# An LSTM over diagonals: x products of short diagonals made together, row buffers kept, two powers in one instruction

## The chip, the cores and the metric

The kernel runs on one core of one Trainium2 chip. The metric is the device time of one execution in microseconds. The kernel before was timed three times: 3999.95, 4003.45 and 4011.36 us, median 4003.45.

TensorE is called PE in the profile (PEld are its weight loads), VectorE is DVE, ScalarE is ACT, GpSimd is POOL and SyncE is SP, which here only issues DMAs. All data is fp32.

## What is computed

The reference takes an image batch of 16 x 64 x 64 positions with 128 features. Layer 0 normalises x over groups of 4 features and runs a two-dimensional LSTM over the 64 x 64 positions; its output is added to x. Layer 1 (attention with landmarks, then a recurrence over tokens) follows and isn't touched by the change. The LSTM step, cut to its core:

```python
f0 = sigmoid(x @ wf0 + bf0 + h_u @ uf0)      # h_u, c_u: the position above
f1 = sigmoid(x @ wf1 + bf1 + h_l @ uf1)      # h_l, c_l: the position to the left
hsum = h_u + h_l
it = sigmoid(x @ wi + bi + hsum @ ui)
ot = sigmoid(x @ wo + bo + hsum @ uo)
cp = tanh(x @ wc + bc + hsum @ uc)
c = f0 * c_u + f1 * c_l + it * cp
h = ot * tanh(c)
```

A position needs those above and to its left, so all positions of one diagonal can be computed at once, and diagonals follow one another.

## The kernel before

**Units.** `lstm_grid` (lines 142 to 372) goes over the 127 diagonals. A diagonal of n positions has 16 n columns (positions times batch); features lie on the 128 partitions. The batch is split in two halves of 8 (`HB`). Up to n = 32 both halves make one unit of 16 n columns; longer diagonals make two units of 8 n columns, so that one half's products can run while the other half's gates are computed. That gives 190 units, numbered 0 to 189 here: units 0 to 31 are diagonals 0 to 31, units 32 to 157 the halves of diagonals 32 to 94, units 158 to 189 diagonals 95 to 126. [...]

**Products.** Each of five gates needs a product with x (`gate_x`, L240) and one with h or with the sum of two h (`gate_h`, L244), added in one PSUM tile `ls_z`. In fp32 a product is two matmul records in the trace, so a unit has ten x records and ten h records. ACT applies the gate's function from `ls_z` (L246).

**Rows of x.** Positions of a diagonal are loaded (`load`, L218) as rows of 128 features, up to 16 positions times 8 images on the 128 partitions, in up to four tiles a unit. Tiles begin at multiples of 16 positions; from diagonal 64 on the first position needed (`lo`) often lies inside a tile, and POOL then clears that tile (L217) before the load, which fills only the rows needed. `enter` transposes the rows on PE (L225), DVE subtracts the group mean (L228) and POOL multiplies by the group's inverse deviation (L232), which gives `ls_xn`, the input of the x products.

**The slot.** The order on every engine is written by hand (`tc.manual_schedule`): `slot(t)` (L319) issues, in this order: the load of unit t + AHEAD (5); h products and gates of unit t; DVE's statistics of the finished rows of unit t - 2 (`measure`, L263, L264); the cell of unit t, with one product on POOL (L330) and the rest on DVE (L329, L331 to L333), tanh on ACT (L334); the transposes of unit t - 1's h back to rows with x added (`turn`, L255, L257); the new h (L338) and the sums of states for the next unit (L236); POOL's factors of unit t - 2 (`factors`, L272 to L282); `enter` of unit t + 2; ACT's normalisation of unit t - 3 (L287) and its stores (L295 on SP); the sum of unit t - 4 for the landmarks (`collect`, L302); the x products of unit t + 1. Each engine runs its part in that order. So on POOL a slot is: L330 of unit t, L272 to L282 of unit t - 2, L232 of unit t + 2, and the clearing (L217) for the next load.

**Factors.** Each row is normalised twice in later layers. `factors` computes, for the k tiles of a unit (2 to 4), the variance plus epsilon (L272), a second value from it (L273), and their powers of -0.5 (L274, L275: a tensor_tensor with the exponents from a constant tile `mhalf`); then, for late units, a mask that zeroes the factor of rows outside the band, one instruction for each such tile (L279), and a bias (L281, L282).

**Before the LSTM** `group_stats` (L34) reads all of x for the group means and deviations. It calls a list of jobs, one an image from the fourth image on: a first job of the attention's tables, the loads of the first units (on ACT's DMA queue), seven more jobs of tables, and at last the turning of a weight (L745 to L750). The 16 images leave room for 13 jobs; there are 12. The last images' statistics end in a short chain over ACT (L81) and POOL (L82, L83) that gives `grstd`.

Of the kernel before, what the change touches and what calls it, by code (L numbers as in the profile page):

```python
# [8 lines left out]
F32 = mybir.dt.float32  # L9
AF = mybir.ActivationFunctionType  # L10
ALU = mybir.AluOpType
# [4 lines left out]
P = 128  # L16
# [4 lines left out]

AHEAD = 5
EPS = 1e-5
# [84 lines left out]
def lstm_tiles(nc, cp, shape, w, u, bias):  # L108

    B, D0, F = shape  # L110
    S = 2
    HB = B // S
    KT = D0 * HB // P
    wt, ut, bt = [], [], []
    for g in range(5):
        a = cp.tile([P, P], F32, name=f"ls_w{g}")
        nc.scalar.dma_start(out=a, in_=w[g])
        wt.append(a)
        a = cp.tile([P, P], F32, name=f"ls_u{g}")
        nc.scalar.dma_start(out=a, in_=u[g])  # L120
        ut.append(a)
        a = cp.tile([P, 1], F32, name=f"ls_b{g}")
        nc.scalar.dma_start(out=a, in_=bias[g].rearrange("(p o) -> p o", o=1))
        bt.append(a)

    hs = [cp.tile([P, S, D0 + 1, HB], F32, name=f"ls_h{k}") for k in range(2)]
    cs = [cp.tile([P, S, D0 + 1, HB], F32, name=f"ls_cell{k}") for k in range(2)]
    for a in (*hs, *cs):
        nc.vector.memset(a, 0.0)
    rows = [cp.tile([P, KT, 2 * F + 4], F32, name=f"ls_tt{k}") for k in range(7)]  # L130
    for a in rows:
        nc.vector.memset(a[:, :, F : F + 4], 1.0)

    later = cp.tile([P, P // HB], F32, name="ls_later")
    nc.gpsimd.memset(later, 1.0)
    nc.gpsimd.affine_select(
        out=later, in_=later, compare_op=ALU.is_ge, fill=0.0, base=0, pattern=[[-HB, P // HB]], channel_multiplier=1
    )
    return wt, ut, bt, hs, cs, rows, later


def lstm_grid(nc, tc, x, fixed, ld, stats, ident, mhalf, gmean, grstd, t1, acc):

# [15 lines left out]
    with ExitStack() as ctx:  # L159
        wt, ut, bt, hs, cs, rows, later = fixed  # L160

# [3 lines left out]
        def unit(t, d, s0, s1):  # L165
# [23 lines left out]
            v.cu, v.cl, v.co = part(before, v.lo), part(before, v.lo + 1), part(now, v.lo + 1)  # L189
            v.tt = rows[t % len(rows)]  # L190
            v.z, v.a = {}, {}
            return v

        def view(v, a):

            return a[:, : v.cols].rearrange("p (s x) -> p s x", s=v.ns)

        def span(v, s, i, c):

            n = (v.hi - v.base) * HB  # L200
            return slice((s - v.s0) * n + (i - v.base) * HB, (s - v.s0) * n + (i - v.base + c) * HB)
# [10 lines left out]
        def load(v, eng=nc.sync):  # L212
            v.xt = ld.tile([P, KT, F], F32, tag="xt", name="ls_xt")
            for k, s, i, c in v.tiles:
                rows, cells = inner(v, i, c)
                if rows.start:
                    nc.gpsimd.memset(v.xt[:, k, :], 0.0)  # L217
                eng.dma_start(out=v.xt[rows, k, :], in_=xv[cells, s * HB : s * HB + HB])  # L218

        def enter(v):  # L220

            xp = ps_t.tile([P, NC], F32, tag="xp", name="ls_xp")
            for k, s, i, c in v.tiles:
                q = c * HB
                nc.tensor.transpose(xp[:, span(v, s, i, c)], v.xt[:q, k, :], ident[:q, :q])  # L225
            v.xn = wk.tile([P, NC], F32, tag="xn", name="ls_xn", bufs=4)[:, : v.cols]
            a = v.xn.rearrange("p (s c b) -> p s c b", s=v.ns, b=HB)
            nc.vector.tensor_tensor(  # L228
                a, xp[:, : v.ns * (v.hi - v.base) * HB].rearrange("p (s c b) -> p s c b", s=v.ns, b=HB)[:, :, v.lo - v.base :],
                norm(v, gmean), ALU.subtract,  # L230
            )
            nc.gpsimd.tensor_tensor(a, a, norm(v, grstd), ALU.mult)  # L232

        def add_states(v):
            v.hsum = view(v, wk.tile([P, NC], F32, tag="hsum", name="ls_hsum"))
            nc.vector.tensor_add(v.hsum, v.hu, v.hl)  # L236

        def gate_x(v, g):
            v.z[g] = ps_z.tile([P, NC], F32, tag="z", name="ls_z")
            nc.tensor.matmul(v.z[g][:, : v.cols], wt[g], v.xn, start=True, stop=False)  # L240

        def gate_h(v, g):
            hin = (v.hu, v.hl)[g] if g < 2 else v.hsum
            nc.tensor.matmul(view(v, v.z[g]), ut[g], hin, start=False, stop=True)  # L244
            a = wk.tile([P, NC], F32, tag=f"g{g}", name=f"ls_g{g}", bufs=3)
            nc.scalar.activation(a[:, : v.cols], v.z[g][:, : v.cols], AF.Tanh if g == 4 else AF.Sigmoid, bias=bt[g])  # L246
            v.a[g] = view(v, a)

# [17 lines left out]
        def factors(v):  # L266
# [6 lines left out]
            nc.gpsimd.tensor_scalar(ve[:, 1, :k], var, 1.0 + EPS, EPS * EPS, ALU.mult, ALU.add)  # L273
            nc.gpsimd.tensor_tensor(v.tt[:, 0:k, F + 2], ve[:, 0, :k], mhalf[:, :k], ALU.pow)  # L274
            nc.gpsimd.tensor_tensor(v.tt[:, 0:k, F + 3], ve[:, 1, :k], mhalf[:, :k], ALU.pow)  # L275
            for j, s, i, c in v.tiles:
                if i < v.lo:
                    f = v.tt[:, j, F + 3 : F + 4]
                    nc.gpsimd.tensor_tensor(f, f, later[:, v.lo - i : v.lo - i + 1], ALU.mult)  # L279
            v.nb = sm.tile([P, KT], F32, tag="nb", name="ls_nb")  # L280
# [24 lines left out]
        for d in range(D0 + D1 - 1):  # L305
# [3 lines left out]
            for s0, s1 in halves:  # L309
# [4 lines left out]
                ready.setdefault(t, []).append(v)  # L314

        def get(t):
            return units[t] if 0 <= t < len(units) else None

        def slot(t):  # L319
            v, p1, p2, p3, p4, after, nxt = (get(t + j) for j in (0, -1, -2, -3, -4, 1, 2))  # L320
            if far := get(t + AHEAD):
# [19 lines left out]
            if p2:  # L341
                factors(p2)
            if nxt:
                enter(nxt)
            if p3:
                normalise(p3)
                store(p3)
            if p4:
                collect(p4)
            if after:  # L350
                for g in (0, 1, 2, 4, 3):
                    gate_x(after, g)

        with tc.manual_schedule(
# [9 lines left out]
            ps_t = ctx.enter_context(tc.tile_pool(name="ls_pst", bufs=1, space=PSUM, reuse_waits="tile"))  # L364
            for t in range(2):
                enter(units[t])
            for r in ready[-1]:
                add_states(r)
            for g in (0, 1, 2, 4, 3):
                gate_x(units[0], g)  # L370
            for t in range(len(units) + 4):
                slot(t)
# [1078 lines left out]
def kernel(ctx: ExitStack, tc: tile.TileContext, ins: dict, out: bass.AP):  # L1451
# [25 lines left out]
    with tc.tile_pool(name="at_c", bufs=1) as ac, tc.tile_pool(name="at_x", bufs=1) as xp, tc.tile_pool(  # L1477
# [4 lines left out]
        with tc.tile_pool(name="first", bufs=1) as first:  # L1482
# [3 lines left out]
            lw = [[ins[f"L0_conv_{k}{g}"] for g in GATES] for k in "wub"]  # L1486
            with tc.tile_pool(name="ls_c", bufs=1) as lc, tc.tile_pool(name="ls_ld", bufs=AHEAD + 4) as ld:
                start = ExitStack()
# [12 lines left out]

                lstm_grid(nc, tc, x, lstm_fixed, ld, stats, ident, mhalf, gmean, grstd, t1, acc)
            rows = [load_rows(nc, xp, t1, 0, g) for g in range(3)]
# [29 lines left out]
```

## Time and profile before

| what | us |
|---|---|
| median of three runs | 4003.45 |
| the profiled execution, its own time | 4009.5 |
| its span | 4008.0 |
| LSTM in the span | about 109 to 1446 |
| PE busy in the span | 3773.7 (94%) |
| POOL busy | 2902.2 (72%) |
| DVE busy | 3012.7 (75%) |
| ACT busy | 2501.7 (62%) |
| POOL's powers L274, 190 instructions | 224.6 |
| POOL's clearing L217, 120 instructions of 0.204 | about 24 |

The span is the time from the first to the last instruction of the profiled execution; 1.5 us of its time lie around it. Rows of instructions in order of time give start, length, engine, line, operation, tile written and tiles read, shape, count, and in brackets the idle time before it with what ended it. Waits are listed as who waited for whom: microseconds in total, times, longest. Rows of matmuls overlap in the profile (their ends are modelled), so short stops of PE show only in the distance between starts.

### The profile page before, as it was taken

The page shows a single profiled execution, that of the slowest core. Times are in us where ns is not written, and L with a number is a line of the kernel's source. Part 1 is how long each engine was busy: PE and PEld are TensorE (multiplying, and loading weights), DVE is VectorE, ACT ScalarE, POOL GpSimd, SP SyncE. Part 2 cuts the span into 40 slices and gives each one's busy share as a digit, 9 for nine tenths or more (in the row PEclk, how much of TensorE's full clock was granted, in tenths as well). Part 3 has the DMA queues.
Part 4 walks back from the last instruction along what each step waited for, and adds up shares of the span by engine and source line. Part 5 has one row for each costly group of instructions (what it writes and reads, how often), then busy time and mean ns, then how long its engine had stood idle before and what let it go on. Part 6 is the DMA issues. An engine that isn't in the chain of part 4 may idle for free. (4 is left out here: it accounts for less than half of the span.)

```text
span 4008.0 us, 98643 instructions
## 1 busy us (share of the span) xinstructions
PE 3773.7 (94%) x36906; PEld 2555.1 (64%) x36906; DVE 3012.7 (75%) x7378; ACT 2501.7 (62%) x5131; POOL 2902.2 (72%) x4440
## 2 busy tenths in 40 slices
PE   7999999999999879889999999999999999988697
PEld 5857655555676669556666666666666666654476
DVE  8689988778888864337788888878888778757465
ACT  0566566566665644346777777677777777645597
POOL 0688877788998954148888888888888888876133
PEclk9899999999999979899999999999999999989799
DMA  9123332323332200113333333333333333223799
GB/s 348 50 73 84 82 82 81 84 83 91 89 86 77 74 17 5 42 28 82 93 85 93 93 86 93 89 88 95 85 91 93 85 95 85 82 65 91 240 266 178
DMA packets 500468, 383.80 MB, mean 96 GB/s; under 512 B 35976, under 2 KB 466960, under 8 KB 499984
## 3 DMA queue, kind: packets, MB, share of 16 engines
q1 hardware_dynamic: 477588, 340.85, 29.5%
q0 software_dynamic: 17728, 34.61, 4.8%
q8 instruction: 294, 4.82, 0.5%
q10 hardware_dynamic: 4668, 1.98, 0.2%
q14 instruction: 190, 1.56, 0.1%
HBM read 172.82 MB, written 204.48 MB: 94 GB/s over the span
## 5 line engine op out<-in xcount | busy, mean ns | idle before, releaser
L984 POOL TENSOR_TENSOR at_total<-at_total,at_e 128x512 f32<-128x512 f32 x480 | 611.6, 1274 | 119.6 <-ACT at_e L957 89.1
L246 ACT ACTIVATE ls_g<-ls_z,ls_b 128x304 f32<-128x304 f32 (+26 forms) x950 | 489.0, 545 | 229.4 <-PE ls_z L244 195.3
L240 PE MATMUL ls_z<-ls_xn,ls_w 128*128 128x304 f32 (+26 forms) x1900 | 607.1, 467 | 8.7 <-POOL ls_xn L232 8.2
L240 PEld LDWEIGHTS ls_z<-ls_xn,ls_w 128*128 128x128 f32 x1900 | 340.4, 196 | 190.7 <-issue 85.7
L851 POOL TENSOR_SCALAR at_T<-at_T,at_nb 128x128 f32<-128x128 f32 x512 | 403.7, 796 | 13.3
L920 DVE TENSOR_REDUCE at_mxq<-at_bank 128x1 f32<-128x512 f32 x512 | 327.6, 682 | 82.6 <-PE at_bank L917 82.4
L244 PE MATMUL ls_z<-ls_hsum,ls_u 128*128 128x304 f32 (+26 forms) x1140 | 371.1, 462 | 0.0
L957 ACT ACTIVATE at_e<-at_bank 128x512 f32<-128x512 f32 x512 | 264.4, 602 | 115.7 <-PE at_bank L951 112.9
L1039 DVE TENSOR_REDUCE at_cmx<-at_bank 128x8 f32<-128x512 f32 x512 | 317.4, 683 | 18.1 <-PE at_bank L1032 14.8
L1068 ACT ACTIVATE at_eT<-at_bank 128x512 f32<-128x512 f32 x512 | 264.4, 602 | 74.4 <-PE at_bank L1065 74.3
L244 PEld LDWEIGHTS ls_z<-ls_hsum,ls_u 128*128 128x128 f32 x1140 | 213.3, 196 | 128.6 <-issue 76.9
L244 PE MATMUL ls_z<-ls_h,ls_u 128*128 128x304 f32 (+26 forms) x760 | 260.6, 466 | 17.3 <-DVE ls_h L338 17.2
L334 ACT ACTIVATE ls_g<-ls_cell 128x304 f32<-128x304 f32 (+26 forms) x190 | 93.2, 491 | 282.1 <-DVE ls_cell L333 278.5
L287 ACT ACTIVATE ls_tt<-ls_tt,ls_nb 128x128 f32<-128x128 f32 (+9 forms) x632 | 261.1, 479 | 5.6 <-POOL ls_nb L282 5.6
L330 POOL TENSOR_TENSOR ls_g<-ls_g,ls_cell 128x304 f32<-128x304 f32 (+26 forms) x190 | 182.1, 958 | 97.7 <-ACT ls_g L246 73.7
L1339 DVE SCALAR_TENSOR_TENSOR rc_y<-rc_w,rc_scale,rc_z 128x256 f32<-128x256 f32 x344 | 155.3, 480 | 108.4 <-PE rc_z L1326 107.0
L274 POOL TENSOR_TENSOR ls_tt<-ls_ve,mhalf 128x4 f32<-128x4 f32 (+2 forms) x190 | 224.6, 1182 | 15.2
L1326 PE MATMUL rc_z<-rc_y,rc_vT 128*128 128x256 f32 x688 | 185.6, 406 | 42.0 <-ACT rc_y L1347 29.6
L1120 ACT ACTIVATE at_z<-at_u,at_nb,at_r 128x128 f32<-128x128 f32 x512 | 211.6, 505 | 11.9 <-POOL at_nb L1115 11.9
L331 DVE TENSOR_TENSOR ls_g<-ls_g,ls_g 128x304 f32<-128x304 f32 (+26 forms) x190 | 98.4, 518 | 159.4 <-POOL ls_g L330 155.5
L1320 POOL DMA_DIRECT2D out_dram<-rc_tt x64 | 77.4, 1209 | 190.5 <-ACT rc_tt L1317 188.6
L244 PEld LDWEIGHTS ls_z<-ls_h,ls_u 128*128 128x128 f32 x760 | 141.6, 196 | 110.3 <-issue 51.0
(262 smaller groups left out, 9696.4 us busy)
## 6 DMA issues: line engine op xcount, KB each, us to landing
t<-ls_tt SPq DMA_DIRECT2D x392, 130.0 KB
at_T<-t SPq DMA_DIRECT2D x128, 264.0 KB
gs_xb<-in_x_dram SPq DMA_DIRECT2D x64, 512.0 KB
at_xh<-t SPq DMA_DIRECT2D x128, 256.0 KB
t<-at_u SPq DMA_DIRECT2D x128, 256.0 KB
out_dram<-at_u SPq DMA_DIRECT2D x128, 256.0 KB
wx<-at_fx SPq DMA_DIRECT2D x128, 256.0 KB
rc_w<-wx SPq DMA_DIRECT2D x64, 512.0 KB
```

Of the source, the lines that this page charges most:

```text
L240: nc.tensor.matmul(v.z[g][:, : v.cols], wt[g], v.xn, start=True, stop=False)
L244: nc.tensor.matmul(view(v, v.z[g]), ut[g], hin, start=False, stop=True)
L246: nc.scalar.activation(a[:, : v.cols], v.z[g][:, : v.cols], AF.Tanh if g == 4 else AF.Sigmoid, bias=bt[g])
L274: nc.gpsimd.tensor_tensor(v.tt[:, 0:k, F + 2], ve[:, 0, :k], mhalf[:, :k], ALU.pow)
L287: nc.scalar.activation(v.tt[:q, k, F + 4 :], v.tt[:q, k, 0:F], AF.Identity, bias=v.nb[:q, k : k + 1], scale=v.tt[:q, k, F + 3 : F + 4],)
L851: nc.gpsimd.tensor_scalar(x[:, c, :], x[:, c, :], gr.nbt[:, 0, c : c + 1], gr.nbt[:, 1, c : c + 1], ALU.mult, ALU.subtract)
L920: nc.vector.tensor_reduce(gr.im.mxq[:, n : n + 1, gr.g], gr.s[n], AX.X, ALU.max)
L957: nc.scalar.activation(gr.e[:, n].rearrange("p c m -> p (c m)"), s[n], AF.Exp)
L984: nc.gpsimd.tensor_tensor(total, total, e[:, :, c, :], ALU.add)
L1039: nc.vector.tensor_reduce(gr.mx[:, n].rearrange("p j c -> p c j"), gr.s[n].rearrange("p (c j m) -> p c j m", c=C, j=2), AX.X, ALU.max)
L1068: nc.scalar.activation(gr.eT[:, n], s[n], AF.Exp)
L1120: nc.scalar.activation(gr.z[:, c, :], gr.u[:, c, :], AF.Identity, bias=gr.nb[:, c : c + 1], scale=gr.r3[:, c : c + 1])
```

## The change

- **x products together.** Neighbouring units whose columns sum to 512 or less are bundled, up to four: diagonals 0 to 3, 4 to 7, 8 to 10, 11 and 12, 13 and 14 at the start; 111 and 112, 113 and 114, 115 and 116, 117 to 119, 120 to 123, 124 to 126 at the end. All other units stay alone. The first unit of a bundle holds the `ls_xn` and `ls_z` tiles for all; its x products are made once for all columns, in the slot before it. Each unit's h product adds to its own columns. So that x is there in time, the units of a bundle enter one in each slot, the last of them two slots before the bundle begins, and loads run 7 units ahead instead of 5. Before the first slot four units enter instead of two; the list of jobs of `group_stats` has one job of loads more, 13 in all.
- **Row buffers kept.** The rows of x go to eleven buffers that are cleared once on POOL before the loop; L217 goes away.
- **Powers.** L274 and L275 become one instruction over both values; the masks of a unit's tiles (L279) become one instruction.

```diff
-AHEAD = 5
+AHEAD = 7
...
+    xs = [cp.tile([P, KT, F], F32, name=f"ls_xt{k}") for k in range(AHEAD + 4)]
+    for a in xs:
+        nc.gpsimd.memset(a, 0.0)
...
         def load(v, eng=nc.sync):
-            v.xt = ld.tile([P, KT, F], F32, tag="xt", name="ls_xt")
             for k, s, i, c in v.tiles:
                 rows, cells = inner(v, i, c)
-                if rows.start:
-                    nc.gpsimd.memset(v.xt[:, k, :], 0.0)
                 eng.dma_start(out=v.xt[rows, k, :], in_=xv[cells, s * HB : s * HB + HB])
...
         def gate_x(v, g):
             v.z[g] = ps_z.tile([P, NC], F32, tag="z", name="ls_z")
-            nc.tensor.matmul(v.z[g][:, : v.cols], wt[g], v.xn, start=True, stop=False)
+            nc.tensor.matmul(v.z[g][:, : v.total], wt[g], v.xn[:, : v.total], start=True, stop=True)

         def gate_h(v, g):
             hin = (v.hu, v.hl)[g] if g < 2 else v.hsum
-            nc.tensor.matmul(view(v, v.z[g]), ut[g], hin, start=False, stop=True)
+            z = v.first.z[g][:, v.off : v.off + v.cols]
+            nc.tensor.matmul(view(v, v.first.z[g]), ut[g], hin, start=False, stop=True, skip_group_check=True)
...
-            nc.gpsimd.tensor_tensor(v.tt[:, 0:k, F + 2], ve[:, 0, :k], mhalf[:, :k], ALU.pow)
-            nc.gpsimd.tensor_tensor(v.tt[:, 0:k, F + 3], ve[:, 1, :k], mhalf[:, :k], ALU.pow)
-            for j, s, i, c in v.tiles:
-                if i < v.lo:
-                    f = v.tt[:, j, F + 3 : F + 4]
-                    nc.gpsimd.tensor_tensor(f, f, later[:, v.lo - i : v.lo - i + 1], ALU.mult)
+            nc.gpsimd.tensor_tensor(
+                v.tt[:, 0:k, F + 2 : F + 4], ve[:, :, :k].rearrange("p r k -> p k r"),
+                mhalf[:, : 2 * k].rearrange("p (k r) -> p k r", k=k), ALU.pow,
+            )
+
+            first = [j for j, s, i, c in v.tiles if i < v.lo]
+            if first:
+                f = v.tt[:, first[0] : first[-1] + 1 : max(first[-1] - first[0], 1), F + 3]
+                r = v.lo - v.base
+                nc.gpsimd.tensor_tensor(f, f, later[:, r : r + 1].to_broadcast([P, len(first)]), ALU.mult)
...
+        while t < end:
+            k = 1
+            while k < 4 and t + k < end and sum(v.cols for v in units[t : t + k + 1]) <= NC:
+                k += 1
+            for j, v in enumerate(units[t : t + k]):
+                v.first, v.off = units[t], sum(p.cols for p in units[t : t + j])
+                if not t:
+                    continue
+                now = entering.setdefault(t + j - k - 1, [[]])
+                if sum(p.ns * (p.hi - p.base) for p in (*now[-1], v)) * HB > NC:
+                    now.append([])
+                now[-1].append(v)
...
-            if nxt:
-                enter(nxt)
+            if t in entering:
+                for vs in entering[t]:
+                    enter(vs)
...
-            if after:
+            if after and after is after.first:
                 for g in (0, 1, 2, 4, 3):
                     gate_x(after, g)
...
-            for t in range(2):
-                enter(units[t])
+            enter(bundle)
             for r in ready[-1]:
                 add_states(r)
             for g in (0, 1, 2, 4, 3):
                 gate_x(units[0], g)
+            for t in range(-AHEAD, 0):
+                for vs in entering.get(t, ()):
+                    enter(vs)
```

## The prediction

> **What bounds the kernel now.** I read the page first, then the busy time of each engine in stretches of the span, then the waits of those stretches, then the order of time. The change touches only the LSTM, which runs from 109 to 1446 us of the span, so that stage alone is priced.
>
> Busy time by stretch (length; PE, PEld, DVE, ACT, POOL; granted clock; DMA):
>
> ```profile
> 109.00:141.00 32.00, 30.81 (x146) 28.42 (x146) 12.81 (x62) 11.47 (x38) 12.49 (x35) 0.52 0.03 7
> ...
> 307.00:540.00 233.00, 232.62 (x942) 160.09 (x942) 219.12 (x616) 139.09 (x329) 193.22 (x289) 1.00 0.32 84
> 540.00:1154.00 614.00, 614.00 (x2096) 348.75 (x2095) 499.95 (x1316) 388.07 (x745) 519.64 (x702) 1.00 0.31 85
> 1154.00:1242.00 88.00, 83.29 (x370) 62.78 (x369) 74.05 (x215) 51.22 (x130) 80.92 (x148) 1.00 0.32 88
> ...
> 1330.00:1425.00 95.00, 78.95 (x450) 64.82 (x448) 74.83 (x262) 58.33 (x161) 86.30 (x208) 1.00 0.24 65
> ```
>
> PE never idles from 540 to 1154 us. POOL is busy 92% of 1154 to 1242 and 91% of 1330 to 1425, where PE does idle. A busy PE hides short stops, because the rows of matmuls overlap; so I also took the starts of PE's rows in order of time. A slot runs from one unit's first h product (L244) to the next's. Its work is ten h records and ten x records (L240) at their usual pitch, plus the transposes at 0.109 us; what is left is a stop. Units are numbered 0 to 189. The stops sum to: units 0 to 5, 1.1 us; 6 to 13, 6.2; 14 to 31, 2.1; 32 to 66, 5.2; 67 to 143, 2.5; 144 to 157 (1154 to 1242 us), 8.5; 158 to 168, 0; 169 to 188 (1330 to 1437 us), 21.6. In all 47 us could be won by removing stops; the rest of the LSTM is PE's own work. Who causes them is in the waits of 1154 to 1242 and then of 1330 to 1437 (total, times, longest):
>
> ```profile
> PEld ls_z L240 <- POOL ls_xn L232: 8.0, 14, 1.0
> ```
> ```profile
> DVE ls_g L331 <- POOL ls_g L330: 18.0, 21, 1.4
> PE ls_z L244 <- DVE ls_h L338: 13.6, 18, 1.0
> ```
>
> In the first stretch PE waits for POOL's normalised x (L232). In the second it waits for the state h, because DVE waits for POOL's product (L330), which stands in POOL's queue behind the factors of an older unit. POOL in order of time there, one unit of 1385 to 1391 us:
>
> ```profile
> 1384.23 0.82 POOL L274 TENSOR_TENSOR ls_tt<-ls_ve,mhalf 128x2 f32<-128x2 f32 x1
> 1385.03 0.88 POOL L275 TENSOR_TENSOR ls_tt<-ls_ve,mhalf 128x2 f32<-128x2 f32 x1
> 1385.99 0.80 POOL L279 TENSOR_TENSOR ls_tt<-ls_tt,ls_later 128x1 f32<-128x1 f32 x2
> ...
> 1387.34 0.74 POOL L232 TENSOR_TENSOR ls_xn<-ls_xn,grstd 128x176 f32<-128x176 f32 x1
> 1388.02 0.34 POOL L217 MEMSET ls_xt<- 128x128 f32 x2
> 1388.32 0.58 POOL L330 TENSOR_TENSOR ls_g<-ls_g,ls_cell 128x192 f32<-128x192 f32 x1
> ```
>
> No idle time stands in front of any of them: POOL sets the pace, and the change shortens just this queue.
>
> **What POOL saves per unit.** No power of 2k elements beside another is in the trace for k = 3 or 4 tiles, but these rows give the price of an element:
>
> ```profile
> L31 POOL TENSOR_TENSOR rc_scale<-rc_ve,mhalf x1: 578/578/578, 3722.9 to 3722.9; 128x1 f32<-128x1 f32 x1
> ```
> ```profile
> L83 POOL TENSOR_TENSOR grstd<-gs_ve,mhalf 128x14 f32<-128x14 f32 x1 | 2.6, 2642 | 0.1
> ```
>
> From 1 to 14 elements: 2064 ns over 13, so 159 ns an element and about 420 fixed. One power less saves the fixed part: for k = 4, 1055 + 1055 against 1690, 0.42 us. From both sides: 0 if a power over two strides (16 bytes apart on the input) costs as much as two, 0.70 to 1.05 us (a whole power of 2 to 4) if elements were free. I take 0.42 and 0.08 of spacing between instructions: 0.5 us a unit.
> [...]
> The cleared rows go too: L217, 0.204 us, one on nearly each of units 96 to 157, two on the short ones after them (120 in all). The masks (L279) of late short units become one of two: 0.80 of the row above falls to about 0.5, alone 0.33 to 0.19. So POOL saves about 0.5 us for early units, 0.67 for late halves, 0.95 for late short ones. The eleven buffers are cleared once, in the first 20 us, when POOL is idle (88.6 us of idle ahead of L73 by the rows of POOL); were that cover gone they'd cost 11 times at most 0.82 (four times L217), 9 us.
>
> **What that is worth, stage by stage.** Units 67 to 143 and 158 to 168: nothing, PE is the bound and its rows don't change. Units 14 to 31: nothing, their stops are the first loads of small transposes. Units 32 to 66: DVE is 94% busy and POOL waits for it (L272 behind L264, 16.3 us), so of 5.2 I take 2. Units 144 to 157: each stop is 0.28 to 0.99, POOL gives 0.67 a slot: 7.5 of 8.5; what is late next is PE itself. Units 169 to 188 by POOL alone: the smaller of the stop and 0.95, summed, 15.9.
> The first x product of a bundle waits for L232 of the bundle's last unit, which enters two slots ahead, as now; the h product queued behind it on PE sees no new wait. Loads issued 7 units ahead go through SP's queue before the same stores as before and read buffers that were read three units ago: no change. Four more of them on ACT's queue at 47 us, 0.65 each, end long before its next work at 64 us.
>
> **What the bundles cost.** For diagonals 0 to 14 and 111 to 126 the x products of 2, 3 or 4 units are made in the slot before the first (eleven bundles, 96 to 496 columns). PE gains only where a record is at its floor, 0.112 us (0.213 at half clock), under about 128 columns. Where it isn't, the same work is bunched: one slot grows and the next can't fall below its chain h product, gates, L330, cell, tanh, h. Chains from rows with POOL's delay taken out: 3.25 us for 8 cells, about 4.5 for 16.
> Late: the slot before unit 174 has 2.95 of other PE work and 10 x 0.416: 7.1 where it took 6.26. Likewise before units 176, 178, 180 and 183: 6.2, 5.3, 5.8, 4.7 against 5.92, 5.05, 4.99, 4.40. Together 2.5 longer instead of 0.95 each shorter: 7.2 lost. After each POOL has caught up, and the next slot falls to its chain: 1.5 more won. The last two slots lose x products at half clock: 1.6 more. Thinner PE work may bring half clock three slots sooner: 2.5 lost. Balance late: 15.9 - 0.2 (a slot counted twice) - 7.2 + 1.5 + 1.6 - 2.5 = 9.
> Early: a fourth load job pushes the turning of the weights (ACT L748 to L750, 0.88 us) from image 14 to image 15, right before ACT L81 on the way to grstd: 0.9 late. Four units enter in place of two before the first x products: two more L232 and their wait, 1.0. These hold 160 columns at half clock, 2.7 against 2.13, and unit 4 enters ahead of the first h product: 0.9 in all. So 2.8 later. Units 0 to 2 then run at their chain, 3.3 instead of 4.7 to 5.2: 5.1 won. The 416 columns behind unit 3 cost 6 us, partly at half clock: 3.4 lost. Units 4 to 6: 2.5 won. The 480, 400 and 464 columns behind units 7, 10 and 12 lose about 4.5, the slots between win 2; half clock at the 480 costs 1.4 more. Balance -2.5.
> [...]
> After the last h (1437 us) three rounds of factors pass POOL alone, 3.1 us each, and landmarks' PE waits 6.43 for the sum behind them: 2 won.
>
> **Sum**: 2 + 7.5 + 9 - 2.5 + 2 = 18 us. The profiled execution took 4009.5 (span 4008.0 and 1.5 around it), so 3991.5 for one like it. That is within the runs shown (3999.95 to 4011.36) and 6 above their median, 4003.45, from which the same 18 give 3985.
>
> **Rivals.** *The bundles eat it*: the short slots after a long one don't fall to the chain (1.5 lost), half clock holds through unit 10 (5.5) and POOL's saving shows half in the tail (5): 5 to 6 us won, 3998. [...]
> *Slower*: the clock stays half through all eleven bundles. Then their 4096 columns take twice 0.0084 us a column, 34 us more, against 18: 4019. It decides from about 2100 columns. Against it: 1.00 granted from 141 to 1425 us, with PE idle a sixth of 1330 to 1425.
> *Elements are free in a power*: 0.3 to 0.6 more per unit where POOL binds, 6 us: 3979.
> *Nothing*: POOL isn't what holds PE, only DVE's neighbour in the wait: 4002. The 92% and 8.0 us of waits for L232 itself speak against it.
>
> **Numbers.** Forecast 3985, 0.54 (12 to 24 us won); bundles 3998, 0.23; free elements 3979, 0.12; nothing 4002, 0.05; slower 4019, 0.06. A difference of 0.3%, 12 us, is about what a measurement tells from none. Faster 0.66, same 0.28, slower 0.06. Range 3972 to 4001: the free elements with bunching that costs nothing (7 us) at one end, nothing won at the other.
>
> **What would show it.** One power row per unit: 1.0 us for two tiles, 1.7 to 2.4 for four. PE's waits for L232 in units 144 to 157 (8.0 us) gone. Slots alternating about 7, 4.6, 6.2, 4.4 from unit 173 on. First h product at 116, not 113.1. Granted clock 0.5 again somewhere in units 4 to 7. Units 67 to 143 at the same pitch. Wrong if a merged power takes over 2.6 us, or if those middle slots move.

## The result and the profile after

The changed kernel took 3999.72 us (median of 19 runs, 3985.96 to 4007.26), the kernel before, beside it, 4007.36 (19 runs, 3994.76 to 4013.78). The ratio is 0.998 with a 95% interval of 0.9971 to 0.999: 8 us faster, where 18 were forecast. The profiled execution has a span of 4000.7 us against 4008.0.

The first view to read is again the busy time by stretch of the changed kernel (columns as before: length; PE, PEld, DVE, ACT, POOL; granted clock; DMA):

```profile
109.00:141.00 32.00, 24.61 (x118) 19.88 (x116) 14.89 (x72) 13.12 (x44) 14.88 (x35) 0.68 0.02 7
...
307.00:540.00 233.00, 231.49 (x938) 159.17 (x937) 219.05 (x609) 138.60 (x327) 186.58 (x249) 1.00 0.31 83
540.00:1154.00 614.00, 614.00 (x2091) 347.73 (x2090) 546.42 (x1318) 388.89 (x745) 492.94 (x574) 1.00 0.31 84
1154.00:1242.00 88.00, 88.00 (x403) 68.25 (x402) 81.52 (x236) 62.07 (x140) 79.14 (x125) 1.00 0.34 92
1330.00:1425.00 95.00, 78.92 (x377) 61.90 (x377) 77.62 (x268) 60.75 (x163) 74.47 (x147) 0.92 0.23 63
```

From 1154 to 1242 us PE is now busy without a break (83.29 of 88 before). From 1330 to 1425 POOL fell from 86.3 to 74.5 us, yet PE's share hasn't moved (78.9 in both), and the clock isn't whole any more. From 307 to 540 PE is busy 1.1 us less than before. From 540 to 1154 DVE took on 46 us (500 to 546) without any new work. The waits say what PE stands behind; first 1154 to 1242 us, then 1330 to 1437 (total, times, longest):

```profile
ACT ls_g L365 <- DVE ls_cell L364: 21.4, 16, 1.8
...
DVE ls_g L362 <- POOL ls_g L361: 0.6, 1, 0.6
```
```profile
PEld ls_z L252 <- DVE ls_h L369: 17.2, 10, 2.3
...
PE ls_z L252 <- DVE ls_h L369: 14.5, 10, 2.0
...
DVE ls_g L362 <- POOL ls_g L361: 5.9, 12, 0.9
...
PE ls_xp L231 <- DVE ls_xn L236: 2.9, 1, 2.9
```

In the first list PE's wait for POOL's normalised x is gone (8.0 us before). In the second, DVE waits for POOL's product 5.9 us instead of 18.0, but PE still waits for h. The last line is new: one single wait of 2.9 us. POOL in order of time, one unit of the same place as before:

```profile
1386.57 0.58 POOL L361 TENSOR_TENSOR ls_g<-ls_g,ls_cell 128x192 f32<-128x192 f32 x1
1387.23 0.22 POOL L280 TENSOR_SCALAR ls_ve<-ls_tt 128x2 f32<-128x2 f32 x1
...
1387.96 1.02 POOL L282 TENSOR_TENSOR ls_tt<-ls_ve,mhalf 128x4 f32<-128x4 f32 x1
1389.07 0.19 POOL L291 TENSOR_TENSOR ls_tt<-ls_tt,ls_later 128x2 f32<-128x2 f32 x1
```

One power of 1.02 us stands where 0.82 and 0.88 stood, one mask where two took 0.80, and no clearing. POOL's part did what it was meant to do.

Where the time went is read from the times of DVE's h rows (L338 before, L369 after), unit by unit. The table has the difference to before within each group of units, in the profiled executions (minus is won); "start" is the h of unit 0, "landmarks" the first product after the LSTM. Behind that the programs are the same, and in the profiled executions that untouched part took from 20 us less to 5 us more than before, so the stages are compared up to there. The last column is the median against that of before in the same set of runs.

| kernel | start | 0-3 | 3-7 | 7-14 | 31-66 | 143-157 | 168-189 | landmarks, sum | median |
|---|---|---|---|---|---|---|---|---|---|
| the change | +5.4 | -5.2 | -0.5 | +6.1 | +1.5 | -7.8 | -2.3 | -4.7 | -7.6 |
| e1 one entry | +5.4 | -5.8 | -0.6 | +6.1 | +1.5 | -7.8 | -6.2 | -9.4 | -11.2 |
| e2 no bundles | +3.1 | 0.0 | -0.3 | -1.2 | +1.5 | -7.8 | -13.6 | -20.3 | -16.0 |
| e3 bundles alone | +5.4 | -5.1 | +0.4 | +4.8 | 0.0 | +0.2 | +2.3 | +8.4 | +6.1 |
| e4 no bundles, 5 ahead | +1.2 | 0.0 | -0.1 | -1.2 | +1.5 | -8.0 | -12.7 | -21.2 | -19.4 |
| e5 = e4, collect later | +0.2 | 0.0 | +1.9 | -0.4 | -1.6 | -4.8 | -9.4 | -16.0 | -20.0 |
| e6 = e4, first bundle | +0.5 | -5.2 | 0.0 | -1.2 | +1.6 | -8.0 | -12.7 | -27.0 | -26.5 |
| e7 one power alone | +0.6 | 0.0 | +1.7 | -1.2 | +1.6 | -6.0 | -6.2 | -11.9 | -14.1 |
| e8 clearing, masks alone | +0.3 | 0.0 | +0.1 | 0.0 | +0.1 | -4.7 | -8.0 | -12.5 | -9.3 |
| e9 = e6 and two edits | +1.5 | -5.2 | -0.1 | -1.2 | -1.7 | -8.0 | -12.7 | -29.2 | -31.1 |
| e10 two bundles, 7 ahead | +4.9 | -5.1 | -1.1 | -0.1 | +1.5 | -7.8 | -13.0 | -22.6 | -22.5 |
| e11 = e2, three load jobs | +2.9 | 0.0 | +1.9 | -1.2 | +1.5 | -7.8 | -12.2 | -16.9 | -17.1 |

In the first row late units won 2.3 us of 9 expected, and by unit 14 the kernel is 5.8 behind where 2.5 were expected. The experiments take these apart.

### The profile page after: what moved, and what is told of

It reads as the page before. It is cut to its first block, busy times and chain, and to the rows that moved or that the text cites. A ratio compares the mean times of both kernels' runs of the same rounds, so it can differ in the third digit from the quotient of the medians.

```text
span 4000.7 us, 98082 instructions
## 1 busy us (share of the span) xinstructions
PE 3759.9 (94%) x36706; PEld 2534.3 (63%) x36706; DVE 3074.8 (77%) x7378; ACT 2510.8 (63%) x5131; POOL 2833.5 (71%) x4111
## 5 line engine op out<-in xcount | busy, mean ns | idle before, releaser
L247 PE MATMUL ls_z<-ls_xn,ls_w 128*128 128x432 f32 (+28 forms) x1700 | 591.3, 495 | 3.9 <-POOL ls_xn L239 3.6
L247 PEld LDWEIGHTS ls_z<-ls_xn,ls_w 128*128 128x128 f32 x1700 | 312.8, 193 | 193.0 <-issue 98.4
L1073 DVE TENSOR_REDUCE at_cmx<-at_bank 128x8 f32<-128x512 f32 x512 | 317.5, 683 | 18.2 <-PE at_bank L1066 12.5
L282 POOL TENSOR_TENSOR ls_tt<-ls_ve,mhalf 128x8 f32<-128x8 f32 (+2 forms) x190 | 314.2, 1654 | 15.8
L239 POOL TENSOR_TENSOR ls_xn<-ls_xn,grstd 128x304 f32<-128x304 f32 (+26 forms) x190 | 202.8, 1068 | 51.1 <-DVE ls_xn L236 48.8
L1154 ACT ACTIVATE at_z<-at_u,at_nb,at_r 128x128 f32<-128x128 f32 x512 | 211.6, 505 | 11.9 <-POOL at_nb L1149 11.9
L1164 ACT COPY at_fx<-at_bank 128x512 f32<-128x512 f32 x128 | 133.0, 1039 | 126.2 <-DVE wx_stats L1162 103.5
```

The source lines that it names most:

```text
L247: nc.tensor.matmul(v.z[g][:, : v.total], wt[g], v.xn[:, : v.total], start=True, stop=True)
L282: nc.gpsimd.tensor_tensor(v.tt[:, 0:k, F + 2 : F + 4], ve[:, :, :k].rearrange("p r k -> p k r"), mhalf[:, : 2 * k].rearrange("p (k r) -> p ...
L1073: nc.vector.tensor_reduce(gr.mx[:, n].rearrange("p j c -> p c j"), gr.s[n].rearrange("p (c j m) -> p c j m", c=C, j=2), AX.X, ALU.max)
L1154: nc.scalar.activation(gr.z[:, c, :], gr.u[:, c, :], AF.Identity, bias=gr.nb[:, c : c + 1], scale=gr.r3[:, c : c + 1])
```

## The experiments

### The slot with two entries (e1)

The single wait of 2.9 us stands in the slot of unit 171, which took 10.7 us against 6.6 before. PE in the changed kernel (idle time in brackets), then DVE:

```profile
1344.21 0.60 PE L231 MATMUL ls_xp<-ident,ls_xt 128*128 128x128 f32 x4
1347.66 0.44 PE L231 MATMUL ls_xp<-ident,ls_xt 128*128 128x128 f32 x2 [2.85 <-DVE ls_xn L236]
1347.93 4.18 PE L247 MATMUL ls_z<-ls_xn,ls_w 128*128 128x288 f32 x10
```
```profile
1346.28 0.48 DVE L369 TENSOR_TENSOR ls_h<-ls_g,ls_g 128x304 f32<-128x304 f32 x1
1346.80 0.46 DVE L243 TENSOR_TENSOR ls_hsum<-ls_h 128x288 f32<-128x288 f32 x1
1347.17 0.43 DVE L236 TENSOR_TENSOR ls_xn<-ls_xp,gmean 128x272 f32<-128x272 f32 x1
```

Units 173 and 174 both enter in this slot: 173 as a single unit two slots ahead, 174 as the first of a bundle of two, three ahead. Together they are too wide for one `ls_xp`, so there are two entries, and `ls_xp` has one buffer. The second entry's transposes wait until DVE has read the first, and DVE does that (L236) only behind the h of unit 171. All of unit 172's x products stand behind those transposes on PE. The granted clock falls too: 0.50 from 1349 to 1351 us, and ten records of 288 columns take 4.18 us here. It is the only slot behind the first h product with two entries. e1 lets the first unit of a bundle of two enter one slot later when the unit ahead stands alone:

```diff
+                late = k == 2 and j == 0 and units[t - 1].first is units[t - 1]
-                now = entering.setdefault(t + j - k - 1, [[]])
+                now = entering.setdefault(t + j - k - 1 + late, [[]])
```

> The changed kernel, but unit 174 enters one slot later (slot 172, together with unit 175, in one tile of PSUM), so that slot 171 has one entry and not two. Theory (two entries in slot 171 go one after the other through the single PSUM buffer ls_xp: the second's transposes wait for the first's subtraction on DVE, and the x products of unit 172 stand behind them on PE): unit 171's slot falls from 10.7 us to about 5.9, the 2.85 us of PE idle before its second transposes goes, granted clock stays 1.00 there, and the total is 4.8 us under the changed kernel's (4.0 to 5.5). Rival (the thin PE work of the bundles and the half clock that follows make this slot long): the slot stays at 9 or more, the total as it was.

Measured: 3997.34 us, ratio 0.9966 (0.9952 to 0.9979). From h of unit 171 to that of 172, e1 takes 0.33 us less than before, where the changed kernel takes 4.05 more; landmarks come 4.7 us earlier than in the changed kernel, 0.8 of it from before unit 14, which the edit doesn't touch. PE in e1 at that place:

```profile
1343.38 0.60 PE L231 MATMUL ls_xp<-ident,ls_xt 128*128 128x128 f32 x4
1343.82 2.59 PE L247 MATMUL ls_z<-ls_xn,ls_w 128*128 128x288 f32 x10
1346.24 1.13 PE L252 MATMUL ls_z<-ls_h,ls_u 128*128 128x288 f32 x4
```

No gap, and the same ten records in 2.59 us. This wait is shown: the slot itself is 4.8 us shorter without it, and the stage behind unit 168 3.9. In the slots of units 172 to 174 0.8 goes again. The clock's fall moved too: granted at half from 1365 to 1368 us in e1, the slot of unit 175 takes 7.88 us against 6.30 in the changed kernel, and that of unit 179 5.66 against 7.34.

### Bundles and POOL's saving apart (e2, e3, e4)

e2 is the changed kernel with every unit a bundle of its own, still 7 units ahead:

```diff
-            while k < 4 and t + k < end and sum(v.cols for v in units[t : t + k + 1]) <= NC:
+            while k < 1 and t + k < end and sum(v.cols for v in units[t : t + k + 1]) <= NC:
```

> The changed kernel without any bundle: every unit makes its x products alone and enters two slots ahead, as in the kernel before; the kept row buffers, the one power and the one mask stay, and loads run 7 units ahead. Theory (POOL's saving is worth what was worked out, and the bundles give most of it back): units 144 to 157 gain 7.5 to 8.5 us against the kernel before, units 169 to 189 about 16, the first h product comes 0 to 3 us later than before, the drain gains 1 to 2: the total is 22 to 27 us under the kernel before, 14 to 19 under the changed one. Rival (POOL's saving is not worth that in the tail: DVE or the chain bind there): 8 to 12 under the kernel before, about as the changed kernel.

Measured: 3992.49 us, ratio 0.9961 (0.9947 to 0.9974). The profiled execution was the shortest of its runs, at 3969.04; that came from the untouched part behind the LSTM.

e3 has the bundles and 7 ahead, with POOL's work as before:

```diff
         def load(v, eng=nc.sync):
...
+                if rows.start:
+                    nc.gpsimd.memset(v.xt[:, k, :], 0.0)
...
-            nc.gpsimd.tensor_tensor(
-                v.tt[:, 0:k, F + 2 : F + 4], ve[:, :, :k].rearrange("p r k -> p k r"),
...
+            nc.gpsimd.tensor_tensor(v.tt[:, 0:k, F + 2], ve[:, 0, :k], mhalf[:, :k], ALU.pow)
+            nc.gpsimd.tensor_tensor(v.tt[:, 0:k, F + 3], ve[:, 1, :k], mhalf[:, :k], ALU.pow)
```

> The changed kernel with POOL's work as in the kernel before: two powers, a mask for each tile, and each late tile cleared before its load (the buffers are the kept ones). Theory (bundles lose): units 144 to 157 as in the kernel before, 5 us lost up to unit 14, the tail about 4 to 10 us longer than in the kernel before; the total is 8 to 15 us over the kernel before. Rival (bundles are what gains): at or under the kernel before.

Measured: 4014.66 us, ratio 1.0007 (0.9995 to 1.002), so by the runs it isn't told from before; its profiled execution has landmarks 8.4 us late. Behind unit 168 it lost 2.3, where 4 to 10 were expected.

e4 is e2 with `AHEAD = 5`:

> No bundles, and loads 5 units ahead as in the kernel before, so that the list of jobs in the statistics has 12 entries again; POOL's savings stay. Theory: as without bundles, but the statistics end where they did in the kernel before: 0.5 us less than with 7 ahead if only the turning of the weights counts, up to 3 if the two more units of loads are what delayed the last image by 2.9 us. Rival (that 2.9 us is chance of the DMAs): the two kernels without bundles agree within 1 us from the first h product on, and their last images come at times that scatter by some 3 us without order.

Measured: 3989.17 us, ratio 0.9948 (0.9934 to 0.9962).

POOL's saving alone is worth 20 to 21 us up to landmarks, less than expected (22 to 27), and the bundles with what they need take some 16 back. The two don't add up: -20.3 (e2) and +8.4 (e3) make -11.9, and the change has -4.7. Most of that is late, where the bundles cost 2.3 alone and 11.3 beside POOL's saving. In e3 the short slots behind the long ones are about 1 us shorter than before (unit 174 takes 5.07 us for 6.09, unit 178 4.17 for 5.45): they remove stops that POOL's saving removes by itself. Late, e2 won 13.6 and e1 6.2, both 7 ahead: even with the double entry mended, bundling costs 7.4 us behind unit 168. Early, the bundles win 5 in units 0 to 3 and give back more in units 7 to 14 and at the start.

### Which bundles lose, and the clock (e6, e10)

e6 is e4 with the bundle of units 0 to 3 alone; e10 has those of 0 to 3 and 4 to 7, 7 ahead:

```diff
-            while k < 1 and t + k < end and ...
+            while k < 4 and t < 1 and t + k < end and ...
```

> The kernel without bundles and 5 units ahead (3989.17 us), with one bundle: units 0 to 3. Theory A: the early loss of 6 us between units 7 and 14 came from the products of 480, 400 and 464 columns, which are no longer there; the first bundle costs 2.1 ahead of the first h product (four units enter, 160 columns at half clock) and wins 5.1 in units 0 to 3: 3 us won, 3986, and the granted clock is 1.00 from 136 us on. Rival: thin h products alone after the first bundle let the clock fall to half again in units 4 to 10, 3 to 6 us lost there: 3989 to 3992, with 0.5 granted somewhere from 140 to 165 us.

Measured: 3979.74 us, ratio 0.9935 (0.9923 to 0.9947). It is as theory A has it: units 0 to 3 won 5.2, the granted clock is 1.00 from 140 us on, and units 3 to 14 are as in e4. From the end of the statistics to the first h product it takes 1.1 us more than e4, where 2.1 were expected; the statistics themselves ended 1.7 us earlier than in e4, for which nothing in the edit gives a reason.

> The changed kernel with the first two bundles alone (units 0 to 3 and 4 to 7, 160 and 416 columns), 7 units ahead. Theory A: the 7 us that units 7 to 14 lost in the changed kernel come from the bundles of 480, 400 and 464 columns behind units 7, 10 and 12: here units 7 to 14 win 1.2 as without bundles. Theory B: they come from the thin slots 4 to 7 (h products only), in which the clock falls to half again: 0.5 is granted somewhere from 140 to 165 us here too, and units 7 to 14 lose 3 or more. The start is late by 2.5 to 3 us as in all kernels with 7 ahead.

Measured: 3989.82 us, ratio 0.9943 (0.993 to 0.9956). Units 7 to 14 take 0.1 less than before. So of the 7.3 us between the change (+6.1) and e6 (-1.2) some 6 come with the bundles of 480, 400 and 464 columns (theory A), and 1.1 with a clock that falls here too (theory B). The slots show how. Those of units 7 to 13 took 7.95, 3.38, 3.90, 7.05, 3.90, 5.97 and 4.26 us in the change, and 5.36, 3.39, 3.91, 4.09, 4.29, 4.48 and 4.68 in e10, where each makes its own x products. Slots 8 and 9 are no shorter without x products than with them: their h products wait for h anyway, and PE does the x products meanwhile. Slots 11 and 13 are 0.4 shorter. Bundled, the x products stand in one piece in front of an h product.

Part of the 6 us is the clock too. Slot 10 takes 7.05 us in the change and 5.40 in e3, which has the same bundles; the stretch from 162 to 164 us lies in that slot, in the change and then in e3:

```profile
162.00:164.00 2.00, 2.00 (x8) 1.87 (x8) 1.18 (x6) 1.32 (x4) 1.30 (x4) 0.50 0.23 58
```
```profile
162.00:164.00 2.00, 2.00 (x15) 1.97 (x15) 1.93 (x8) 1.75 (x6) 1.83 (x5) 1.00 0.15 39
```

With these 1.65 us, theory B has some 2.8 of the 7.3 and theory A some 4.5; that is an estimate, as POOL does more in e3. The clock of e10, by stretch (granted clock is the third figure from the end), then PE's rows there:

```profile
132.00:136.00 4.00, 4.00 (x18) 2.52 (x16) 0.63 (x4) 0.49 (x4) 0.23 (x1) 0.92 0.10 29
136.00:140.00 4.00, 2.18 (x18) 1.62 (x17) 3.26 (x15) 3.06 (x12) 3.08 (x9) 1.00 0.01 4
140.00:144.00 4.00, 1.71 (x14) 1.56 (x14) 3.64 (x15) 2.54 (x9) 2.99 (x8) 0.86 0.14 41
144.00:148.00 4.00, 3.50 (x16) 3.41 (x17) 3.29 (x14) 3.02 (x10) 3.25 (x8) 0.50 0.17 51
```
```profile
137.91 0.69 PE L252 MATMUL ls_z<-ls_h,ls_u 128*128 128x96 f32 x4 [1.31 <-DVE ls_h L369]
...
141.13 0.70 PE L252 MATMUL ls_z<-ls_h,ls_u 128*128 128x112 f32 x4 [1.65 <-DVE ls_h L369]
...
144.50 1.22 PE L252 MATMUL ls_z<-ls_h,ls_u 128*128 128x128 f32 x4 [1.66 <-DVE ls_h L369]
```

Behind idle stretches of 1.31 and 1.65 us, with 1.6 us of work between them, the clock falls to half (0.86 granted from 140 to 144 us, the fall at 142.9). After a third of 1.66 us four records of 128 columns take 1.22 us, where e6 at the whole clock has 0.71.

### The loss of units 32 to 66 (e5, e9)

All kernels with the merged power lost 1.5 to 1.6 us there, unless collect was moved; e3 and e8, with two powers, lost none, and e7, with the merged power alone, lost 1.6: it is the power. The sum for the landmarks (collect, L302 before, L314 after) is the one instruction that grew. Before, on DVE and on POOL:

```profile
313.80 0.75 DVE L302 TENSOR_TENSOR acc<-acc,ls_tt 128x256 f32<-128x256 f32 x2
```
```profile
314.28 0.89 POOL L232 TENSOR_TENSOR ls_xn<-ls_xn,grstd 128x272 f32<-128x272 f32 x1
```

And in e4, the same unit:

```profile
312.19 0.43 DVE L364 TENSOR_TENSOR ls_cell<-ls_g,ls_g 128x264 f32<-128x264 f32 x1
...
314.35 1.31 DVE L314 TENSOR_TENSOR acc<-acc,ls_tt 128x256 f32<-128x256 f32 x2
```
```profile
311.95 1.73 POOL L282 TENSOR_TENSOR ls_tt<-ls_ve,mhalf 128x8 f32<-128x8 f32 x1
...
314.51 0.87 POOL L239 TENSOR_TENSOR ls_xn<-ls_xn,grstd 128x272 f32<-128x272 f32 x1
```

The pair of sums took 0.75 us when POOL's multiply began 0.48 behind its start, and 1.31 when it began 0.16 behind: the second sum then ends some 0.28 after the multiply. POOL, quicker by one power, comes just then. DVE is 95% busy in these slots, so it counts. The whole loss lies in the slots of units 31 to 33 (0.55, 0.57 and 0.44 us), where the lengths of the two sums add up to 0.83 us before and 1.38 to 1.40 in e4; in those of units 36 to 44 they add up to some 1.3 in the kernel before as well. From 540 to 1154 us, where PE sets the pace, 106 collects have a mean of 512 ns before and some 790 after, 30 of DVE's 46 us more, and it costs nothing.

What makes the sums take longer beside the multiply, these rows don't show. Not every instruction of POOL does it: during the power's 1.73 us DVE's L364, also of two inputs, takes its usual 0.43.

e5 is e4 with collect behind the statistics of the next slot, beside POOL's small factor instructions:

```diff
             if p2:
                 measure(p2)
+            if p5:
+                collect(p5)
...
-            if p4:
-                collect(p4)
```

> The kernel without bundles and 5 units ahead (3989.17 us), with the collecting sum of a unit moved on VectorE from ahead of the next unit's statistics to behind them. Theory: units 32 to 66 lost 1.5 us in all kernels in which GpSimd saves, because GpSimd now reaches its multiply of x just when VectorE adds the two rows of collect, and those two then take 1.30 us where they took 0.75; VectorE is 95% busy there. Moved, collect stands beside GpSimd's small factor instructions: the pair is back at 0.75, units 32 to 66 win 1.5 or more against the kernel without this move, in all 3987.5 us or a little less. In units 67 to 143 collect's mean falls from about 790 towards 510 ns and no time comes of it, as TensorE sets the pace. Rival: the loss of 1.5 comes from the wait of the x products for GpSimd itself, whatever collect does, or collect meets GpSimd's other product in its new place: units 32 to 66 stay 1.5 longer than before, 3989 or more.

Measured: 3986.28 us, ratio 0.995 (0.9937 to 0.9962). Units 32 to 66 won 3.1 against e4 and are 1.6 faster than before. Most of it isn't the loss coming back: the slots of units 31 to 33 are still 0.6 longer than before, with the two sums at 0.78 to 0.94 us, and the slots of units 34 to 65 are 2.2 shorter. So the meeting with POOL's multiply is shown for 0.9 of the 1.5 us; what holds the other 0.6 is open. In units 67 to 143 collect's mean is 526 ns against 792 without the move (e6). But units 143 to 157 won only 4.8 of 8.0 and late units 9.4 of 12.7: there collect stands in front of the cell's first product. e9 moves it in slots 32 to 70 alone, on top of e6, and carries a second edit at the end of the statistics:

```diff
+            if p5 and 32 <= t <= 70:
+                collect(p5)
...
         spread(first, nc.scalar.copy)
+        warm(8)
         centre(last, nc.vector.tensor_copy, nc.vector)
+        warm(6)
         spread(last, nc.vector.tensor_copy)
```

`warm(n)` is n transposes of a constant tile into a PSUM tile of the statistics that nobody reads.

> The kernel with the first bundle alone (3979.74 us) with two further edits that show in different stages. First: 8 and 6 transposes of a constant 128x128 tile, whose result nobody reads, in TensorE's gaps of 1.3 and 0.9 us at the end of the group statistics, where the granted clock falls from 1.00 to 0.5 at 108 to 109 us. Theory of the prediction (narrow products alone keep the clock at half): the clock still falls, a few us later at most, and h of unit 7 comes at most 2 us earlier. Rival (only an idle stretch lowers it): 1.00 from 104 to 150 us, and units 0 to 6 win 5 to 9 us. Second: in slots 32 to 70 alone collect stands behind the statistics. Theory: units 32 to 66 return to the time of before (1.6 us won against the kernel without), and units 143 to 157 keep their 8 us. In all 3978 by the first theory, 3971 by the rival.

Measured: 3981.21 us beside 4012.34 of before, ratio 0.9924 (0.9912 to 0.9936), the lowest ratio of all, though its interval overlaps with that of e6. Units 32 to 66 took 1.7 us less than before, and units 143 to 157 kept their 8. Groups of collect in the stretch of 307 to 345 us (count, total us, mean ns), of before, e4 and e9 in this order:

```profile
L302 DVE TENSOR_TENSOR acc<-acc,ls_tt 128x256 f32<-128x256 f32 (+6 forms) x13 | 6.7, 552 | 0.0
```
```profile
L314 DVE TENSOR_TENSOR acc<-acc,ls_tt 128x256 f32<-128x256 f32 (+6 forms) x13 | 8.4, 683 | 0.0
```
```profile
L321 DVE TENSOR_TENSOR acc<-acc,ls_tt 128x256 f32<-128x256 f32 (+5 forms) x11 | 5.3, 520 | 0.0
```

The transposes did nothing for the clock (e9, by stretch):

```profile
104.00:108.00 4.00, 3.41 (x29) 3.00 (x30) 3.54 (x7) 1.45 (x2) 1.22 (x2) 1.00 0.14 40
108.00:112.00 4.00, 1.93 (x18) 1.60 (x18) 1.50 (x10) 0.00 (x0) 3.61 (x7) 0.76 0.02 4
112.00:116.00 4.00, 4.00 (x17) 4.00 (x18) 0.17 (x1) 0.56 (x3) 0.09 (x1) 0.50 0.00 0
```

PE is busy 3.41 of the first 4 us, against 1.55 in e6, and the clock still falls at 110 us; at 112 to 116 it is at half with PE busy 4.00 of 4 in products of 160 and 16 columns. One idle stretch of 1.85 us stayed: from 110.0 us on PE waits for POOL's x. So filling the gaps ahead of it isn't enough, but idle time as the cause isn't ruled out. What wide work inside units 0 to 6 would do wasn't tried.

### POOL's two savings (e7, e8) and the start (e11)

e7 is the kernel before with the one power for two; e8 is e4 with two powers (so only the clearing and the masks are changed).

> The kernel before with one edit: the two powers of a unit in one instruction. Theory: GpSimd saves some 0.4 to 0.5 us a unit; units 32 to 66 lose 1.5 as in the others (there is no clearing there, so it must come from the power), units 144 to 157 win 5 to 6 of 8.5, units 169 to 188 win 5, the drain 1: landmarks' first product about 10 us earlier, 3998 us. Rival: the 1.5 of units 32 to 66 isn't the power's; or a power of 8 hides nothing because GpSimd starts later on its first result: units 144 to 157 win under 3, 4003 or more.

Measured: 3992.14 us, ratio 0.9964 (0.9952 to 0.9976).

> The kernel without bundles and 5 units ahead, with the two powers as before: only the clearing of rows and the masks are left of the change. Theory: units 32 to 66 as before (0), units 144 to 157 win about 4 (0.28 a slot with its spacing, 14 slots), units 169 to 188 win 9 to 11 (two clearings and one mask, 0.65 to 0.75 a unit), the drain 1: landmarks' first product some 15 us earlier, 3994 us. If both savings come out of one queue that is full, the two wins together are about the 21 us of both edits; if one saving alone already takes GpSimd off the path, they sum to clearly more than 21.

Measured: 3996.97 us, ratio 0.9973 (0.9963 to 0.9983). In units 143 to 157 the parts won 6.0 and 4.7, both together 8.0: PE itself is the limit there, as 8.5 us of stops had said. Late they won 6.2 and 8.0, together 12.7: the second saving finds part of the wait gone already.

e11 is e2 with the first loads in three jobs, so that the turning of the weights is back at image 14:

```diff
-[... units[a : min(a + 2, AHEAD)]] for a in range(0, AHEAD, 2)]
+[... units[a : min(a + 3, AHEAD)]] for a in range(0, AHEAD, 3)]
```

> The kernel without bundles and 7 units ahead (3992.49 us), with the first loads in three jobs of 3, 3 and 1 units in place of four of 2, 2, 2 and 1, so that the turning of the weights is back at the last image but one. Kernels with 7 ahead had the last image's statistics 2.5 to 3.1 us later than before, those with 5 ahead 0.9 earlier to 0.9 later. Theory of the prediction: the turning of the weights (a job later) is what delays the end of the statistics: here the last image comes within 1 us of before. Rival: the two more units' loads on the DMA queues are it: still 2 to 3 us later.

Measured: 3995.29 us, ratio 0.9953 (0.9941 to 0.9965). The last image's statistics still come 2.43 us later than before (2.47 in e2). So it isn't the turning. What 7 ahead brings are two more units' loads: from 96 to 104 us the DMA engines are busy for 1.02 of their time in e11, 0.85 in before, but that may be the later images themselves. By their own count the packets on the loads' queue are only 0.3% of the share up to 108 us more (7.2 against 6.9 before, some 0.3 us); why the images end 2.4 later stays open.

## Why the prediction was right in direction and wrong in size

The profile's reading held: POOL set the pace in units 144 to 157 and behind 169, and in units 144 to 157 its saving is worth what the bound of the stops allowed. What failed are sums on the other side, and the late saving in part. Term by term, up to landmarks:

| term | forecast | measured |
|---|---|---|
| units 32 to 66 | 2 won | 1.5 lost |
| units 66 to 143 | 0 | 1.0 won |
| units 144 to 157 | 7.5 won | 7.8 won |
| late, POOL alone | 15.9 won | 13.6 won (e2; 12.7 in e4) |
| late, bundling | 6.8 lost | 7.4 lost (e2 to e1) |
| late, slot of unit 171 | not seen | 3.9 lost (e1 to the change) |
| start | 2.8 later | 5.4 later |
| units 0 to 3 | 5.1 won | 5.2 won |
| units 3 to 7 | 0.9 lost | 0.5 won |
| units 7 to 14 | 3.9 lost | 6.1 lost, POOL's 1.2 won inside |
| drain | 2 won | 1.0 won |

**The step that failed most is "Balance late: ... = 9"**; 2.3 came. It priced each slot by PE's records and looked only at the slot before each bundle, the longer ones. It didn't go through which units enter where, although the change moves that too, and so missed the double entry in the slot of unit 171, which isn't the slot before a bundle: 3.9 of the 6.7 missing. Most of the rest is the 15.9: it took the smaller of the stop and POOL's saving in each slot and added them, as if nothing else had been close behind. In e2, without bundles, PE still waits 8.3 us for h behind unit 168, while DVE waits only 1.2 for POOL (13.6 and 18.0 before), so the chain of h itself came next:

```profile
PE ls_z L252 <- DVE ls_h L369: 8.3, 16, 0.9
...
DVE ls_g L362 <- POOL ls_g L361: 1.2, 4, 0.6
```

The bunching was right within 0.6 us as a sum, and the first slots came as forecast: those of units 173 to 176 took 7.11, 4.62, 6.30 and 4.36 us for about 7, 4.6, 6.2 and 4.4. The 2.5 for half clock was placed wrong: it was put at the end, and the clock also fell in between (0.72 granted from 1388 to 1392 us; the slot of unit 179 took 7.34 us, 5.66 in e1). That thin work by itself brings half clock, as the 2.5 and the 1.4 at the 480 suppose, no run shows: in the kernel before 1.00 was granted from 1410 to 1420 us in products of 80 to 112 columns, and in the changed kernel the clock fell with idle stretches of PE beside it, of 1.72 and 1.77 us around 144 us and of 2.02 up to 1389.7. That the sum is so close is partly luck.

**"Balance -2.5" early** was -5.8. Units 0 to 3 came out as worked out from their chain. "The slots between win 2" came: those of units 8, 9, 11 and 13 took 1.9 us less than before, though POOL's saving alone gives 0.7 of it (e4). What failed is the price of the three bundles: the slots of units 7, 10 and 12 took 8.2 us more than before, with 5.9 forecast (4.5, and 1.4 for half clock at the 480). The second fall of the clock, 1.65 in the slot of unit 10, wasn't in the sum. The start was out by 2.6, with the first h product at 118.4 us: the four entries and the first x products took 1.3 and 1.2 more (1.0 and 0.9 forecast), but the end of the statistics came 2.9 later (0.9 forecast), and not for the turning of the weights: with that put back (e11) the delay is the same. All kernels with 7 ahead have it, and its cause stays open.

**"Of 5.2 I take 2" in units 32 to 66** had the sign wrong. The row showed DVE at 94% and POOL waiting for it; a quicker POOL could gain little there, and its multiply moved onto collect in three slots, which explains 0.9 of the loss.

The rivals: *the bundles eat it* was the closest (3998), but that it fits so well is luck. Its half clock was right in a milder form: 0.50 from 144 to 150 us and 0.71 from 162 to 166, not all through. The short slots behind the long ones did get shorter, POOL's saving in the tail was far more than half, and the double entry wasn't in it. *Elements are free in a power* is ruled out: in the changed kernel a power of eight elements has a mean of 1.96 us and one of four 1.07, some 220 ns an element where the prediction has 159. For k = 4 the two powers before had means of 1.39 and 1.28, above the 1.055 of the prediction, so 0.71 us a unit was saved and not 0.42; in units 144 to 157 the stops left no room for more. *Slower* and *nothing* didn't come.

## What to carry to other kernels

When a change moves the order in which work enters, go through every slot and list what stands in it, not only the slots that the change is about: one slot with two users of a single buffer cost 3.9 us, about half as much as the whole change won. Work off the chain is hardly saved by being made together where it filled idle time between two links of the chain for nothing; bunched, it stands in front of a link, and in the slots left thin PE idled and the clock fell (0.50 granted from 144 to 148 us in e10). Only the first bundle, of very narrow products, paid (5.2 us). When one engine gets faster, look at what the neighbour does at the moment to which its instructions move.

## What the runs showed of the hardware that was not expected

- Two DVE sums of 128x256 took 0.75 us or 1.31, by whether POOL's multiply of 128x272 began 0.48 or 0.16 us after them. In e6 collect's mean in units 67 to 143 is 792 ns, in e5 526.
- The clock fell to half after two idle stretches of PE of 1.31 and 1.65 us with 1.6 us of work between them (e10; 0.86 granted from 140 to 144 us, 0.50 from 144 to 148), and stayed at half (0.50 granted) from 112 to 140 us in the kernel before with PE busy 4.00 of every 4 us in products of 16 to 96 columns. The length of one stretch doesn't tell the cases apart: the clock was at half behind one of 1.88 us in the change (at 160.8 us) and whole behind one of 2.15 in e3 (at 162.0 us).
- The moment at which it rises varied between executions of the same early work: between 140 and 144 us in before, e2, e4 and e8, at 146 to 147 in e5 and e7 and 150 in e11 (whose LSTM starts 2.9 later than before). These three lost 1.7 to 1.9 us in units 3 to 7, where their work is that of e2 and e4.
